# The last batch's contexts, output and writes stand behind the experts

## The chip, the cores and the metric

One core of a Trainium2 chip runs the whole program. The metric is device time in microseconds (us) of one execution; shown are the median of several executions and their range. One further execution was recorded by the hardware profiler, and every duration below comes from it. Engines: TensorE (PE) multiplies matrices, VectorE (DVE) and ScalarE (ACT) work on elements, GpSimd (POOL) here mostly issues indirect DMAs, SyncE (SP) issues the loads of weights. An indirect DMA takes or writes rows of a table in HBM by a list of row numbers; one form of it adds to the rows that are there.

## The reference

Four decoder layers on x of 8 batches with 100 tokens of 512 numbers, each layer an attention to a context of 361 tokens per batch and a feed-forward block. The change touches only the last layer, L3: a linear attention with 16 heads of 32, and 16 experts of inner size 352, four for each token. The expert numbers cover tokens 0 to 511 only, so the tokens from 512 on get nothing from the experts.

```python
q_prime = relu(einsum('bhnd,fd->bhnf', q, Wqf))
k_prime = relu(einsum('bhnd,fd->bhnf', k, Wkf)) * attention_mask[:, None, :, None]
kv  = einsum('bhnf,bhne->bhfe', k_prime, v)
qkv = einsum('bhmf,bhfe->bhme', q_prime, kv)
out = qkv / (einsum('bhmf,bhf->bhm', q_prime, sum(k_prime, axis=2))[..., None] + 1e-08)
x   = x + (out.transpose(0, 2, 1, 3).reshape(B, Sq, H) @ Wo.T + bo)
...
xs   = layernorm(x)[tok]                       # rows sorted by expert
down = (silu(xs @ gate[e].T) * (xs @ up[e].T)) @ down[e].T
x    = x + zeros.at[tok].add(down * w_sorted[:, None])
```

## The kernel before

x stays on the chip as seven tiles of 128 rows (800 tokens; the last tile has 32). Within a batch the rows are sorted by a key of the first layer, so `home` holds for each row the token it belongs to, and whatever leaves the chip by token is written by an indirect DMA, the helper `scatter` (line 2133). `home_far` holds the tokens of rows 600 to 639. Tokens 512 and up need no expert; as sorting stays within a batch, the first six batches (600 rows, `T3P`) hold all tokens that do. Row 600 lies in tile 4, whose first 88 rows (`NEAR`) belong to batch 5.

`linear_attention` runs a loop over the batches. In step b it makes keys and values of batch b (`kv_pieces`, 4 key and 3 value pieces), their features (`features`, VectorE operation kp, line 1858), and for batch b-1 `sums` (k'v and the sum of k'), `turned` (four transposes of it and a copy) and `attend`. `attend` is 64 small matmuls, then on VectorE an addition, a reciprocal and two products (lines 1919 to 1922), which overwrite qT with the contexts. After the contexts comes the product with the output weight `wo`, four products of 128 x 512 to a tile (the trace counts eight matmul records), and an addition to x (`out_to_x`, line 229). In step 7 the tiles of the first 512 rows get their output, then tile 4 for its first 88 rows only (`out_part(0)`; a column of ones and zeros decides which rows count, line 1942). `spread_normal` then normalises the five tiles into y and scatters y to the table `normal` in HBM, and x to the output. The buffers of y are two. A ninth step finishes batch 7 (turned, attend), the other 40 rows of tile 4 and tiles 5 and 6, and three scatters write them. All of the attention's TensorE work is held in the written order (`in_order`); other engines and DMAs are ordered by a planner, which puts what is ready first at the front of an engine's queue. Every queue then runs in order: an instruction that waits holds all behind it.

`routed_experts` goes over the 16 experts, `widen` of expert e+1 ahead of `narrow` of expert e. Each expert has 152 places in two halves of 76. `widen` loads the gate and up weights (704 KB each, line 90, four buffers `w`, shared with the attention's four weights), gathers the rows from `normal` by two indirect DMAs (xs, line 2163, three buffers), transposes them and makes 48 matmuls. `narrow` loads the down weight (768 KB, line 96, two buffers `v`), makes 48 matmuls, turns the result back, scales it (o, line 2213), and adds it to the output by two indirect DMAs with addition (line 2215). The two of one expert touch different rows; an expert's pair waits until the pair of the expert before has landed, since a token has several experts. A conditional block behind the experts handles more than 152 places of an expert.

Of the kernel before, what the change touches and what calls it, by code (L numbers as in the profile page):

```python
# [22 lines left out]
F32 = mybir.dt.float32  # L23
# [7 lines left out]
T = NB * LQ  # L31
# [28 lines left out]
def decoder_kernel(ctx: ExitStack, tc: tile.TileContext, a: dict, out: bass.AP):  # L60
# [50 lines left out]
    @contextmanager  # L111
    def in_order():
        pinned[0] = True
        yield
        pinned[0] = False
# [44 lines left out]
    NEAR = T3P - NT3 * 128  # L160
    assert T3P + 128 - NEAR <= T3P + LQ
    home_far = const.tile([128 - NEAR, 1], I32, name="home_far")

    def gather_x(src):
        for t, rows in TILES:
# [101 lines left out]
    def window_attention():  # L267
# [7 lines left out]
        with ExitStack() as st:  # L275
# [18 lines left out]
            with tc.tile_pool(name="l0s", bufs=1) as sp, tc.tile_pool(name="l0c", bufs=2) as cp, in_order():  # L294
# [141 lines left out]
                for t, rows in TILES:  # L436
# [5 lines left out]
                    p3[: 128 - NEAR, NTT : NTT + 1],  # L442
                    [(perm.rearrange("p b q -> p (b q)")[:, T3P : T3P + 128 - NEAR], iota_p[:LQ])],
                )
                ahead = sp.tile([128, NTT, NB - 1], F32, name="ahead")
                nc.gpsimd.iota(
                    ahead,
# [10 lines left out]
                nc.vector.tensor_tensor(home[:rows, t, :], batch[:rows, t : t + 1], p3[:rows, t : t + 1], ALU.add)  # L458
                nc.vector.tensor_scalar(
                    home_far, p3[: 128 - NEAR, NTT : NTT + 1], float(T3P), None, ALU.add  # L460
                )
                gather_x(a["x"])

# [1316 lines left out]

    def linear_attention(ctxT, first_done):

# [2 lines left out]
        F = 64  # L1789
        JP = KD // 2  # L1790
        halves = [slice(i * F, (i + 1) * F) for i in range(2)]
        with ExitStack() as st, in_order():
            res = st.enter_context(tc.tile_pool(name="a3", bufs=1))
            wq, wk, wv, wo = weights_of("a3_w")
            bqk = res.tile([128, 2, KD], F32, name="bqk")
# [3 lines left out]
            nc.sync.dma_start(out=feat, in_=a["a3_feat"])  # L1799
            mask = res.tile([128, NB, 3], F32, name="mask")  # L1800
            nc.sync.dma_start(out=mask, in_=a["mask_ff"])
            kvp = st.enter_context(tc.tile_pool(name="a3k", bufs=2))

            def of_head(m, g):

# [61 lines left out]
            def sums(b):  # L1867

                kp, va = kps.pop(b), kv.pop(b)[1]
                p = ps1()  # L1870
                n = KD * F
                for j in range(KD):
                    for c, (_, kn) in enumerate(KCH):
                        for g in range(4):
                            matmul(
                                p[four_heads(g), j * F : (j + 1) * F],
                                lhsT=va[:kn, c, j * 4 + g, :],
                                rhs=kp[:kn, c, g, j, :],
                                start=c == 0,
                                stop=c == 2,  # L1880
                            )
                for c, (_, kn) in enumerate(KCH):
                    for g in range(4):
                        matmul(
                            p[four_heads(g), n : 2 * n],
                            lhsT=ones[:kn, 0:HD],
                            rhs=kp[:kn, c, g, :, :].rearrange("p j f -> p (j f)"),
                            start=c == 0,
                            stop=c == 2,
                        )  # L1890
                sT = hp.tile([128, 4, 128], F32, name="sT")
                nc.scalar.copy(sT.rearrange("p i n -> p (i n)"), p)
                return sT

# [8 lines left out]
            def attend(b, z):  # L1903
                toks = slice(b * LQ, (b + 1) * LQ)
                p = ps2()
                for m in range(2):
                    for jp in range(JP):
                        for i, part in enumerate(halves):
                            for g in range(4):
                                c0 = (m * JP + jp) * LQ  # L1910
                                matmul(
                                    p[four_heads(g), i, c0 : c0 + LQ],
                                    lhsT=z[part, m, jp, four_heads(g)],
                                    rhs=qp[part, jp, g, toks],
                                    start=True,
                                    stop=True,
                                )
                rl = hp.tile([128, 2, JP * LQ], F32, name="rl")
                nc.vector.tensor_scalar(rl, p[:, :, JP * LQ : 2 * JP * LQ], 1e-8, None, ALU.add)
                nc.vector.reciprocal(rl, rl)  # L1920
                for i in range(2):
                    nc.vector.tensor_tensor(  # L1922
                        qT[:, i::2, toks],
                        p[:, i, : JP * LQ].rearrange("p (j q) -> p j q", j=JP),
                        rl[:, i, :].rearrange("p (j q) -> p j q", j=JP),
                        ALU.mult,
                    )
# [1 line left out]
            woks = [wo[:, k, :] for k in range(KD)]  # L1929


            counts = res.tile([128, 2], F32, name="counts")
            nc.gpsimd.iota(
                counts, pattern=[[0, 2]], base=-NEAR, channel_multiplier=1, allow_small_or_imprecise_dtypes=True
            )
            for i, op in enumerate((ALU.is_lt, ALU.is_ge)):
                nc.vector.tensor_scalar(counts[:, i : i + 1], counts[:, i : i + 1], 0.0, None, op)

            def out_part(i):
                p = ps1()  # L1940
                mm(p, [(qT[:, k, NT3 * 128 : NT3 * 128 + 128], w) for k, w in enumerate(woks)])
                nc.vector.scalar_tensor_tensor(
                    x[:, NT3, :], p, counts[:, i : i + 1], x[:, NT3, :], ALU.mult, ALU.add
                )

            for b in range(NB + 1):
                if 0 < b < NB:
                    kv[b] = kv_pieces(kvp, ctxT, b, wk, wv, bqk[:, 1, :], bv)
                keys, values = (kv[b][2][0::2], kv[b][2][1::2]) if b < NB else ([], [])
                if b == 0:  # L1950
                    keys = []
                    values[1:] = [lambda v=values[1:3]: (v[0](), due.pop()(), v[1]())]
# [3 lines left out]
                    sT = sums(b - 1)  # L1956
                if b == NB - 1:
                    out_to_x(qT, woks, TILES[:NT3])
                    out_part(0)
                    first_done()  # L1960
                if b == NB:
                    out_part(1)
                for part in keys[2:]:
                    part()
                if b:
                    z = turned(sT)
                for c in range(3):
                    if b < NB:
                        features(b, c)
                    for part in values[c : c + 1]:  # L1970
                        part()
                if b:
                    attend(b - 1, z)
            out_to_x(qT, woks, TILES[NT3 + 1 :])
            scatter(flat, home_far, x[NEAR:, NT3, :])
            for t, rows in TILES[NT3 + 1 :]:
                scatter(flat, home[:rows, t, :], x[:rows, t, :])

# [149 lines left out]
    def scatter(dst, at, src):  # L2130
# [5 lines left out]
        )  # L2136
        for other in writes[:-1]:
            tc.declare_no_dep(writes[-1].ins, other.ins, reason="each token has its own row")

    def spread_normal():  # L2140

        tiles = [(t, min(128, T3P - t * 128)) for t in range(NT3 + 1)]
        with tc.tile_pool(name="f3y", bufs=2) as yp:
            stats = norm_stats(x, NT3 + 1)
            for t, rows in tiles:
                y = yp.tile([128, D], F32, name="y")
                normed(y, x, stats, t)
                scatter(normal, home[:rows, t, :], y[:rows, :])
            for t, rows in tiles:
                scatter(flat, home[:rows, t, :], x[:rows, t, :])  # L2150

    def routed_experts():
        with ExitStack() as st:
            hp = st.enter_context(tc.tile_pool(name="f3h", bufs=2, reuse_waits="tile"))

            def widen(e):

                wg, wu = (
                    load_w(a["f3_gu"][e, i])[:, : KD * I3].rearrange("p (k n) -> p k n", k=KD) for i in range(2)
                )  # L2160
                xs = hp.tile([SH, 2, D], F32, name="xs", bufs=3)
                for h in range(2):
                    nc.gpsimd.indirect_dma_start(
                        out=xs[:, h, :],
                        out_offset=None,
                        in_=normal,
                        in_offset=bass.IndirectOffsetOnAxis(ap=r_tok[:, e, h : h + 1], axis=0),
                    )
                xT = hp.tile([128, KD, SLOTS], F32, name="xT")
                for h in range(2):  # L2170
                    p = ps1()
# [22 lines left out]
            def narrow(e, hT):  # L2194
# [11 lines left out]
                evac(oT.rearrange("p (i k) s -> p i (k s)", i=2), p[:, :, : 2 * SLOTS])  # L2206
                o = hp.tile([SH, 2, D], F32, name="o", bufs=4)
                adds = []
                for h in range(2):
                    p = ps1()  # L2210
                    for d in range(KD):
# [8 lines left out]
                            compute_op=ALU.add,  # L2220
                        )
                    )
                tc.declare_no_dep(adds[1].ins, adds[0].ins, reason="an expert's slots have different rows")

            skewed(range(E3), widen, narrow)


        with tc.If(nc.values_load(n_over, min_val=0, max_val=E3 * T3) > 0), ExitStack() as st:
            res = st.enter_context(tc.tile_pool(name="f3o", bufs=1))
            hp = st.enter_context(tc.tile_pool(name="f3p", bufs=2))  # L2230
# [43 lines left out]
            again()  # L2274

    window_attention()
    with ExitStack() as later:
        begun = []

        def follow(between):  # L2280
# [6 lines left out]
        ctxT = begun[0]  # L2287
        softmax_attention(ctxT)
        gated_ffn()
        linear_attention(ctxT, spread_normal)  # L2290
    routed_experts()

# [137 lines left out]
```

## Time and profile before

| what | us |
|---|---|
| median of 3 runs (range) | 2076.41 (2071.13 to 2076.53) |
| profiled execution, device time | 2075.22 |
| its span, first to last instruction | 2073.4 |
| TensorE busy in the span | 1903.3 (92%) |
| VectorE, ScalarE, GpSimd busy | 834.3, 523.5, 228.7 |
| last product of the attention ends (1846.41 + 8.80) | 1855.2 |
| first matmul of expert 0 | 1863.81 |
| last transposes of expert 15 begin | 2042.36 |
| indirect DMA with addition: from issue to landing, smallest, median, largest | 7.0, 7.9, 13.9 |
| gather of xs: from issue to landing, median | 6.8 |

Three views are used. The table by stage gives busy time of each engine in a stretch; it shows which engine is full and where none is. The timeline lists instructions with the idle time before them and what ended it. The chain of waits follows the last instruction back to what it waited for. A wait for several things is shown under the one that ended last.

### The profile page before, as it was taken

What the parts mean: (1) busy time and instruction counts of PE and PEld (TensorE: products, weight loads), DVE (VectorE), ACT (ScalarE), POOL (GpSimd) and SP (SyncE); (2) the same over time, 40 slices, a digit from 0 to 9 for tenths busy, and PEclk for the clock granted to TensorE, in tenths of its full rate; (3) what the DMA queues carried; (4) which work ended last, traced back from release to release, by engine and by line L of the source; (5) the groups of instructions that cost most, each with busy time, mean ns of one, the idle gap of its engine ahead of it and who ended that gap; (6) DMA issues with size and microseconds to landing.
All of it is one profiled execution on the core that took longest, in us unless ns stands there. A gap on an engine that the chain in (4) does not pass through costs nothing.

```text
span 2073.4 us, 28880 instructions
## 1 busy us (share of the span) xinstructions
PE 1903.3 (92%) x12202; PEld 1127.2 (54%) x12202; DVE 834.3 (40%) x1567; ACT 523.5 (25%) x1150; POOL 228.7 (11%) x197
## 2 busy tenths in 40 slices
PE   6999999889989999578999999999998999979993
PEld 4676665433345555234555554555444555539993
DVE  4354444543343364774455564111113333332221
ACT  1243323234214433262344441001001111001110
POOL 4100000123200000201000000000001000124452
PEclk8999999999989999799999999999998999989997
DMA  9600000468902221300000010111021000027883
GB/s 274 203 23 19 31 21 2 187 246 258 357 22 82 82 82 42 117 1 11 21 1 1 1 42 21 46 56 41 21 81 21 1 2 2 27 88 215 257 255 58
DMA packets 61565, 171.99 MB, mean 83 GB/s; under 512 B 18840, under 2 KB 27332, under 8 KB 54640
## 3 DMA queue, kind: packets, MB, share of 16 engines
q1 hardware_dynamic: 35122, 135.37, 18.8%
q0 software_dynamic: 21296, 25.42, 5.3%
q10 hardware_dynamic: 5006, 9.22, 1.3%
q8 instruction: 100, 1.64, 0.3%
q14 instruction: 41, 0.34, 0.1%
HBM read 146.10 MB, written 19.55 MB: 80 GB/s over the span
## 4 chain that ended last, share of the span: by engine, by line
PE 48%; issue 15%; DVE 8%; DMA 6%; ACT 3%; POOL 1%; POOLq 0%; DVEq 0%; ACTq 0%; SPq 0%
PE ps L102 45%; PE ps L107 3%; DMA out_x<-o,r_row 2%; ACT sc L1683 1%; DMA got<-back,where_i 1%; ACT pT L1425 1%; DMA read<-table 1%; DVE amax L1579 1%; DVE va L1299 1%; DMA ctxT<-in_ctxT 1%; DVE y L196 1%; DVE pT L1420 1%; DVE sc L1688 0%; POOL sent L1084 0%; DVE nmx L1680 0%
## 5 line engine op out<-in xcount | busy, mean ns | idle before, releaser
L102 PE MATMUL ps<-yT,w 128*128 128x400 f32 x768 | 267.1, 510 | 0.0
L102 PE MATMUL ps<-w,ctxT 128*128 128x512 f32 (+1 forms) x576 | 264.9, 603 | 0.0
L102 PE MATMUL ps<-ctxT,w 128*128 128x361 f32 x768 | 251.1, 475 | 0.0
L102 PEld LDWEIGHTS ps<-yT,w 128*128 128x128 f32 x768 | 148.5, 194 | 115.0 <-issue 8.6
L102 PEld LDWEIGHTS ps<-ctxT,w 128*128 128x128 f32 x768 | 142.3, 190 | 91.6 <-issue 17.5
L102 PEld LDWEIGHTS ps<-w,ctxT 128*128 128x128 f32 (+1 forms) x576 | 102.7, 184 | 118.6 <-issue 109.8
L1291 ACT ACTIVATE kT<-ps,bqk 128x361 f32<-128x361 f32 x96 | 53.6, 559 | 227.3 <-PE ps L102 226.1
L1299 DVE TENSOR_TENSOR va<-ps,r_a_bv 128x512 f32<-128x512 f32 (+1 forms) x72 | 49.7, 690 | 143.1 <-PE ps L102 143.1
L102 PE MATMUL ps<-xT,w 128*128 128x152 f32 (+1 forms) x768 | 104.4, 297 | 1.2 <-issue 0.6
L102 PEld LDWEIGHTS ps<-xT,w 128*128 128x128 f32 (+1 forms) x768 | 100.8, 183 | 2.6 <-issue 0.8
L229 DVE TENSOR_TENSOR x<-x,ps 128x512 f32<-128x512 f32 (+1 forms) x52 | 35.7, 686 | 138.9 <-PE ps L102 138.9
L102 PE MATMUL ps<-w_vo,oc 128*128 128x512 f32 (+1 forms) x224 | 90.5, 598 | 0.0
L917 DVE TENSOR_TENSOR hT<-sg,ps 128x400 f32<-128x400 f32 x36 | 20.6, 571 | 163.3 <-PE ps L102 161.1
L102 PE MATMUL ps<-w,qT 128*128 128x512 f32 (+1 forms) x176 | 79.0, 606 | 4.8 <-DVE qT L1922 4.8
L1683 ACT ACTIVATE sc<-ps,nmx 100x361 f32<-100x361 f32 x128 | 70.2, 561 | 50.2 <-DVE nmx L1680 50.2
L107 PEld LDWEIGHTS ps<-ident,sc 100*128 100x128 f32 (+1 forms) x512 | 54.5, 153 | 39.4 <-issue 25.1
L1425 ACT ACTIVATE pT<-pT,mbi,msc 128x800 f32<-128x800 f32 (+1 forms) x48 | 47.9, 1046 | 103.4 <-DVE pT L1420 103.4
L2215 POOL DMA_INDIRECT out_x<-o,r_row x32 | 59.0, 1844 | 100.2 <-DMA out_x<-o,r_row 58.0
L631 ACT ACTIVATE sc<-sc,nmx 100x128 f32<-100x128 f32 x128 | 49.8, 390 | 79.4 <-DVE nmx L628 78.4
L107 PE MATMUL ps<-ident,sc 100*128 100x100 f32 (+1 forms) x512 | 63.6, 261 | 5.3 <-DVE va L1299 3.9
L2119 POOL DMA_DIRECT2D read<-table x1 | 3.5, 3487 | 568.0 <-issue 568.0
L102 PE MATMUL ps<-v,hT 128*128 128x512 f32 (+1 forms) x140 | 61.8, 593 | 0.0
(377 smaller groups left out, 2763.9 us busy)
## 6 DMA issues: line engine op xcount, KB each, us to landing
w<-in_f_gu SPq DMA_DIRECT2D x32, 704.0 KB, 6.7
wd<-in_f_dn SPq DMA_DIRECT2D x32, 512.0 KB, 6.0
v<-in_f_w SPq DMA_DIRECT2D x16, 1024.0 KB, 6.0
w<-in_a_w SPq DMA_DIRECT2D x12, 1024.0 KB, 6.5
v<-in_f_dn SPq DMA_DIRECT2D x16, 768.0 KB, 8.7
w<-in_f_gu SPq DMA_DIRECT2D x9, 1024.0 KB, 4.8
gu<-in_f_gu SPq DMA_DIRECT2D x8, 1024.0 KB, 18.4
cx<-in_ctxT SPq DMA_DIRECT2D x8, 722.0 KB, 12.8
```

The costliest lines, as they stand in the source:

```text
L102: ins = nc.tensor.matmul(dst, **args)
L107: ins = nc.tensor.transpose(dst, src, unit)
L196: nc.vector.tensor_scalar(dst, src[:, t, :], mv[:, t, 0:1], rstd[:, t : t + 1], ALU.subtract, ALU.mult)
L229: nc.vector.tensor_tensor(x[:rows, t, :], x[:rows, t, :], p[:rows, :], ALU.add)
L631: nc.scalar.activation(sc[:, g, :], sc[:, g, :], AF.Exp, bias=nmx[:, g : g + 1], accum_out=l[:, g : g + 1])
L1291: ins = nc.scalar.activation(kT[:, m, :], p[:, :LK], AF.Identity, bias=bk[:, m : m + 1])
L1299: ins = nc.vector.tensor_tensor(va[:kn, c, :, 0:HD], p[:kn, :].rearrange("p (h d) -> p h d", d=HD), bv[:kn, :].rearrange("p (h d) -> p h d ...
L1420: nc.vector.tensor_scalar(dst, s[i][:kn, :, : KD * LQ], LIM * root, -LIM * root, ALU.min, ALU.max)
L1425: nc.scalar.activation(dst, dst, AF.Exp, bias=mbi[:kn, b, c : c + 1], scale=msc[:kn, b, c : c + 1])
L1579: nc.vector.tensor_reduce(amax, src, AX.X, ALU.max, apply_absolute_value=True)
L1683: nc.scalar.activation(sc[:, h, :], s[i][:LQ, g, :LK], AF.Exp, bias=nmx[:, g : g + 1], accum_out=l[:, h : h + 1])
L2215: nc.gpsimd.indirect_dma_start(out=flat, out_offset=bass.IndirectOffsetOnAxis(ap=r_row[:, e, h : h + 1], axis=0), in_=o[:, h, :], in_offse ...
```

## The change

1. The ninth step leaves the attention. A new function `rest` does batch 7's `turned` and `attend`, the rows of batch 7 in tile 5, tile 6, and their writes. It is called in `narrow` of expert 15, ahead of that expert's last transposes and adding writes. It loads `wo` a second time.
2. Tile 5 holds the end of batch 6 (rows up to 700, 60 rows of the tile: `HEAD`) and the beginning of batch 7. Its output product is now done twice, once for each part of the rows, as tile 4's already was, and it is written in two parts; `home_last` holds the tokens of the second part. One small matmul and one VectorE operation at the start make it; two more small columns choose the rows.
3. `sums` of batch 7, the second part of tile 4, the first part of tile 5 and their writes stay ahead of the experts.
4. The gathers of experts 0 and 1 are traced right after batch 6's contexts, ahead of these writes (`ask`). The gather of expert e+2 is traced in `widen` of expert e. xs has two buffers instead of three, in a pool opened before the attention.
5. y is written into the two buffers `v`, four tiles to a buffer, in place of two buffers of its own.
6. The pools move: the attention's tiles stay until the experts end; the pool of keys and values and the experts' pool lie on the other side of the memory, the latter where the context was. sT and rl have one buffer instead of two.
7. Dependencies: the moved writes and the adding writes are declared independent, as no expert's row is of the last batch; the last pair keeps its wait for the pair before it.

```diff
-            for b in range(NB + 1):
-                if 0 < b < NB:
+            for b in range(NB):
+                if b:
                     kv[b] = kv_pieces(kvp, ctxT, b, wk, wv, bqk[:, 1, :], bv)
...
-                    out_part(0)
+                    out_part(0, 0)
                     first_done()
-                if b == NB:
-                    out_part(1)
...
-            out_to_x(qT, woks, TILES[NT3 + 1 :])
+            ask()
+            sT = sums(NB - 1)
+            out_part(0, 1)
             scatter(flat, home_far, x[NEAR:, NT3, :])
-            for t, rows in TILES[NT3 + 1 :]:
-                scatter(flat, home[:rows, t, :], x[:rows, t, :])
+            out_part(1, 0)
+            scatter(flat, home[:HEAD, TL, :], x[:HEAD, TL, :])
+
+        def rest():
+            with in_order():
+                wo = load_w(a["a3_w"][3]).rearrange("p (k n) -> p k n", k=KD)
+                woks = [wo[:, k, :] for k in range(KD)]
+                attend(NB - 1, turned(sT))
+                out_part(1, 1, woks)
+                out_to_x(qT, woks, TILES[TL + 1 :])
+            done = [scatter(flat, home_last, x[HEAD:, TL, :])]
+            for t, rows in TILES[TL + 1 :]:
+                done.append(scatter(flat, home[:rows, t, :], x[:rows, t, :]))
+            return done
...
     def spread_normal():
-        with tc.tile_pool(name="f3y", bufs=2) as yp:
-            stats = norm_stats(x, NT3 + 1)
-            for t, rows in tiles:
-                y = yp.tile([128, D], F32, name="y")
+        stats = norm_stats(x, NT3 + 1)
+        two = [vpool.tile([128, 2048], F32, tag="v", name="v") for _ in range(2)]
+        for t, rows in tiles:
+            y = two[t // 4][:, t % 4 * D : (t % 4 + 1) * D]
...
-                xs = hp.tile([SH, 2, D], F32, name="xs", bufs=3)
-                for h in range(2):
-                    nc.gpsimd.indirect_dma_start(
...
+                xs = asked.pop(0)
+                if e + 2 < E3:
+                    asked.append(fetch(e + 2))
...
                 evac(oT.rearrange("p (i k) s -> p i (k s)", i=2), p[:, :, : 2 * SLOTS])
                 o = hp.tile([SH, 2, D], F32, name="o", bufs=4)
                 adds = []
+                others = rest() if e == E3 - 1 else []
...
+                    for other in others:
+                        tc.declare_no_dep(adds[h].ins, other.ins, reason="no expert's row is of the last batch")
+                        for before in all_adds[-2:]:
+                            tc.add_manual_dep(
+                                adds[h].ins,
+                                before.ins.name,
+                                mybir.DependencyInfo(mybir.DependencyClass.Sync, mybir.DependencyReason.DATA),
+                            )
...
-        linear_attention(ctxT, spread_normal)
-    routed_experts()
+        fetch = rows_of(last.enter_context(tc.tile_pool(name="f3x", bufs=2)))
+        asked = []
+        rest = linear_attention(ctxT, last, spread_normal, lambda: asked.extend(fetch(e) for e in range(2)))
+        later.close()
+        routed_experts(last, fetch, asked, rest)
```

`fetch(e)` allocates xs and issues the same two gathers as before.

## Prediction, made before the changed kernel was built

> **What bounds the kernel now.** I read the table by stage first, over the end of the last layer. Columns: stretch, its length, busy time of TensorE (PE) with count, weight loads, VectorE (DVE), ScalarE (ACT), GpSimd (POOL), granted TensorE clock, DMA share, GB/s.
>
> ```profile
> 1820.00:1840.00 20.00, 18.44 (x272) 9.82 (x273) 10.06 (x14) 0.58 (x1) 1.88 (x2) 0.91 0.18 60
> 1840.00:1860.00 20.00, 11.12 (x89) 4.37 (x87) 5.98 (x7) 0.61 (x2) 6.15 (x6) 0.91 0.21 64
> 1860.00:1880.00 20.00, 16.32 (x116) 16.03 (x117) 2.21 (x6) 3.29 (x7) 8.03 (x8) 0.83 0.51 154
> 1940.00:1960.00 20.00, 19.97 (x158) 19.59 (x158) 4.44 (x10) 2.47 (x7) 11.39 (x8) 1.00 0.87 240
> 2040.00:2060.00 20.00, 2.54 (x20) 2.05 (x18) 2.34 (x4) 0.00 (x0) 7.26 (x4) 0.69 0.24 33
> ```
>
> TensorE is full up to 1840, has a hole at the hand-over from attention to experts (1840 to 1864), is full again through the experts, and stands still from about 2043 while POOL goes on. So two places are open: the hole, and the tail. The timeline of the hole (start, duration, engine, line, operation, tiles, count, idle before and who ended it):
>
> ```profile
> 1815.30 0.55 DVE L196 TENSOR_SCALAR y<-x,mv,rstd 128x512 f32<-128x512 f32 x1 [2.72 <-DMA normal<-y,home]
> 1819.11 0.55 DVE L196 TENSOR_SCALAR y<-x,mv,rstd 128x512 f32<-128x512 f32 x1 [3.27 <-DMA normal<-y,home]
> 1820.37 0.44 PE L102 MATMUL ps<-feat,kT 32*128 32x64 f32 x4 [1.45 <-DVE kp L1858]
> ...
> 1836.68 3.70 PE L102 MATMUL ps<-w,qT 128*128 128x512 f32 x8 [0.97 <-DVE qT L1922]
> 1840.21 0.60 PE L107 MATMUL ps<-ident,sT 128*128 128x128 f32 x4
> 1846.41 8.80 PE L102 MATMUL ps<-w,qT 128*128 128x512 f32 x16 [3.85 <-DVE qT L1922]
> 1852.74 0.98 POOL L2133 DMA_INDIRECT out_x<-x,home  x1 [10.36 <-DVE x L229]
> 1854.02 1.16 POOL L2163 DMA_INDIRECT xs<-normal,r_tok  x1 [0.30 <-issue]
> 1862.45 0.74 PE L107 MATMUL ps<-ident,xs 76*128 76x76 f32 x4 [2.51 <-DMA xs<-normal,r_tok]
> ```
>
> The rows of the first expert are asked for only at 1854.02, behind a write that waited 10.36 us for x. Expert 0's first matmul follows at 1863.81. In the tail, POOL's timeline shows the pairs of adding writes (L2215), one pair per expert, and the chain of waits ends on them:
>
> ```profile
> 1909.19 1.86 POOL L2215 DMA_INDIRECT out_x<-o,r_row  x1 [6.29 <-DMA out_x<-o,r_row]
> 1923.88 1.86 POOL L2215 DMA_INDIRECT out_x<-o,r_row  x1 [7.78 <-DMA out_x<-o,r_row]
> 1939.36 1.87 POOL L2215 DMA_INDIRECT out_x<-o,r_row  x1 [8.58 <-DMA out_x<-o,r_row]
> 2051.44 1.82 POOL L2215 DMA_INDIRECT out_x<-o,r_row  x1 [6.33 <-DMA out_x<-o,r_row]
> 2062.22 1.84 POOL L2215 DMA_INDIRECT out_x<-o,r_row  x1 [6.84 <-DMA out_x<-o,r_row]
> ```
>
> Each expert's pair waits until the pair before has landed. The sixteen pairs start from 1884.81 to 2062.22: 15 periods in 177.4 us, mean 11.83. TensorE's period per expert is 11.0 (transposes of o at 1949.21, 1960.38, 1971.22). The periods after experts 1, 2 and 3 are 13.2, 14.7 and 15.5; from expert 4 on the mean is 11.2. So the pairs fall about 10 us behind o (o of expert 4 at 1927.81, its pair at 1939.36) and stay there. Call that lag D. At the end the adds alone last from 2043 to 2073.4. The end is therefore first pair + 15 periods + the last landing (2073.4 - 2062.2 = 11.2).
>
> **The change, part by part.**
>
> *The normalised rows.* y now has room for all five tiles, so the 2.72 and 3.27 us for which VectorE waited on a landed write go. Behind them in VectorE's queue stood kp, and for kp TensorE stood 1.45 + 0.22 us (1820.37, 1821.03). Gain 0 to 1.7; I take 1.5, as the row names the cause. The price: y borrows the two buffers in which the down weights of experts 0 and 1 were loaded long before. Both loads (768 KB each) now wait for the writes of normal, about 1822, land 9 to 11 us later, and are needed at 1879.06 - 20. The attention's last 20 us and expert 0 cover them: nothing. Without this cover one load, some 10 us, would show once.
>
> *The hole.* Four gathers (1.45 us apart on POOL) now stand behind the writes of normal (last issued 1821.74, landed some 3.2 us later), so about 1825 to 1831. A gather lands in 4.8 us on a quiet DMA and at worst 12.1 in this trace: 1843 at the latest. POOL's writes of x behind them wait for VectorE until 1841 anyway. TensorE keeps its work up to the half product ending at 1840.3, adds the half of the tile in which batch 7 begins (8 matmuls, 3.70) up to 1844.0, and transposes the rows at once; from the second transposes to the first matmul it was 1.36 (1862.45 to 1863.81). First matmul of expert 0: 1845.4 instead of 1863.81, **18.4 earlier**. If the gathers stood behind the write waiting for 1841.47, they would land near 1849 and 5 of it were lost. The second weight of expert 1 waits for the buffer of the output weight, issued at 1855.24; its buffer now comes free at 1844, 11 earlier, and lands 6.7 later, before expert 1 at about 1853. Expert 0's matmuls took 7.84 at clock 0.83, later ones 6.44: with a shorter hole 0 to 1.4 come back; I take 0.6. So the first pair of adds moves by 18.4 + 1.5 + 0.6 = **20.5**; bounds 13 and 21.5.
>
> *Two buffers of rows instead of three.* The gather for expert e+2 now needs the buffer of expert e, free after its transposes. On POOL it stands behind the pair of e-2, as the gather for e+3 does now (1896 pair 1, 1900.30 gather for 6 by the three buffers). What is queued behind the waiting pair is thus the gather for four experts later, and TensorE waits for it. Its second half starts 4.3 + 1.45 us after the pair begins and lands after L. The rows are wanted two periods and 0.35 after o: slack = 22.65 - 1.05 - D - 5.75 - L = 15.8 - D - L. L has medians of 5.6 to 10 in windows over the experts. With D = 10 and L = 7 the slack is -1.2: TensorE will stall a little at most experts from about the eighth on. That alone costs nothing, since the pairs, not o, set the end; it lowers D. But D fixes where a pair falls against the burst of weight loads: pairs starting 2.9 to 4.2 us after a burst (bursts at 1935.13, 1946.35, 1968.37) had periods of 10.3 to 11.9, those near its start (1923.88 against 1924.28) 15.5. Cost: from nothing to 12 periods at 13 (+22); I take +0.4 for eight periods, **+3**, being nearest to the rows at 2.9.
>
> *The work behind the experts.* Transposes, contexts and two output tiles lasted 1840.21 to 1856.0, 15.8 us, most of it waiting (reciprocal 2.65, clock 0.82 in the 8.80). It is the same work plus, on POOL, one more write than before (0.95 + 0.3): tile 5 is written in two parts, and two writes stand ahead of the last pair. It begins after expert 15's last product, 2041.4 on the old clock, and its writes are issued by 2041.4 + 15.8 + 2 = 2059.2. The last pair waits for its forerunner until 2062.2. So 3 us of cover are left, and TensorE's stalls come off it: 0 to 5; I take 0.5. The second load of the output weight (1 MB, 6.5 us) takes the buffer that comes free at 2024: 10 us early, nothing. Without the lag D, these 15.8 us would all stand on the path.
>
> *At the start* one more matmul and one VectorE operation, and a few on small tiles: 0 to 0.4 us, I take 0.2.
>
> **A rule against it.** For a SWDGE transfer (issued by GpSimd) the Trainium skill, "DMA: Bandwidth & Descriptors", section "Anatomy of one DMA — SWDGE (gpsimd) path", gives 2.0 us plus bytes over 436 GB/s. For 76 rows of 2 KB that is an estimate of 2.4 us. The pairs here land in 7.0 to 13.9 us, median 7.9. By the rule pairs would never lag, the cover in the tail would not exist, and the end would be o of expert 15 plus the 15.8 us: the moved work would come back in full, and of the gain 20.5 - 15.8 - 2 = 2.7 us would be left. The measurement decides here.
>
> **The sum.** Span 2073.4 - 20.5 + 3 + 0.5 + 0.2 = 2056.6. The profiled execution took 2075.22, so 1.8 lie around the span, and the median of the runs is 2076.41, 1.2 above it: **2060**. Own range 2052 to 2068.
>
> **The rivals.**
> - *The pairs stop lagging.* In an undisturbed order the periods equal TensorE's 11.0 from the start, and the tail is TensorE's: 2041.4 - 20.5 + 15.8 + 2 + 11.2 = 2049.9, with 3.0 around it 2053. For it: expert 4's pair and later have 11.2. Against: three of the first four periods are long. Chance 0.12.
> - *The gathers come late at the start, and the moved work shows in the tail.* 13 instead of 20.5 gained, 5 exposed: 2073.4 - 13 + 3 + 5 + 3 = 2071; it does only half of what it says. For it: POOL's queue is in order, and here a write waiting for x held the gathers. Against: nothing they need is later than 1825. Chance 0.12; half of it lies within the noise.
> - *Slower: the two buffers tie TensorE to the adds.* Each gather sits behind a pair that waits for a landing; if stalls pull D down to 6, pairs meet the weight bursts and the period stays at the 13.2 to 15.5 of experts 1 to 3. At a mean of 14.2 the 15 periods take 213 instead of 177.4: 2073.4 - 20.5 + 35.6 + 3 = 2091.5. It decides from a mean period of (177.4 + 20.5 + 6.2)/15 = 13.6. Against: a longer period leaves the DMA more time between bursts, and shortens L. Chance 0.11.
>
> **How the numbers follow.** Forecast 0.65, the others 0.12, 0.12, 0.11. A measurement tells about 0.3% (6 us) from no change. Faster: 0.65 + 0.12 + 0.06, less 0.03 for the forecast's own longest stalls, 0.80; within 0.3% 0.09; slower 0.11. The range runs from 2051 to 2076: below it lies part of the first rival, above it the slower one and the worst of the second.
>
> **What would show it.** Right: the first gather issued before 1835 and the first expert's matmul at 1842 to 1847; no VectorE wait on the writes of normal; TensorE waiting 0.5 to 3 us for xs at several later experts; pairs with a mean period of 11.5 to 12.2; the contexts, output and three writes done before the last pair. Wrong: gathers behind the write to out_x at 1841; mean periods above 13; the last pair waiting for VectorE or for the moved writes instead of for its forerunner. What would break the forecast is the phase of adds against weight loads, which I only read from single periods.

## The result, and the profile after

The changed kernel is faster by 0.7%: median 2056.66 us (2052.87 to 2068.04, 10 runs) against 2076.1 (2064.31 to 2077.41, 10 runs) of the kernel before. The ratio is 0.9934, with a 95% interval of 0.9912 to 0.9956. The profiled execution has a span of 2051.1 (before 2073.4), 22.3 less.

The table by stage of the changed kernel (columns as before):

```profile
1820.00:1840.00 20.00, 18.75 (x254) 9.80 (x253) 8.91 (x12) 1.37 (x3) 5.77 (x6) 1.00 0.52 154
1840.00:1860.00 20.00, 19.15 (x154) 18.85 (x155) 3.10 (x8) 3.39 (x8) 5.31 (x6) 1.00 0.69 227
1860.00:1880.00 20.00, 20.00 (x159) 19.66 (x157) 4.54 (x10) 2.40 (x7) 11.87 (x8) 1.00 0.71 191
2020.00:2040.00 20.00, 11.16 (x24) 4.10 (x24) 6.52 (x8) 0.00 (x0) 7.50 (x5) 0.82 0.26 42
```

The hole at 1840 to 1864 is gone: TensorE is busy 19.15 of 20 us there, at clock 1.00 instead of 0.91 and 0.83. The work that stood in it now shows in 2020 to 2040. The timeline of the hand-over:

```profile
1810.53 2.53 DVE L199 TENSOR_SCALAR v<-x,mv,rstd 128x512 f32<-128x512 f32 x5
1820.96 1.17 POOL L2186 DMA_INDIRECT xs<-normal,r_tok  x1 [3.25 <-issue]
1826.99 1.02 PE L102 MATMUL ps<-qp,z 64*32 64x100 f32 x64
1831.76 7.13 PE L102 MATMUL ps<-w,qT 128*128 128x512 f32 x16 [0.60 <-DVE qT L1933]
1836.57 0.95 POOL L2160 DMA_INDIRECT out_x<-x,home_far  x1 [10.14 <-DVE x L1955]
1838.73 0.69 PE L107 MATMUL ps<-ident,xs 76*128 76x76 f32 x8
1840.24 6.44 PE L102 MATMUL ps<-xT,w 128*128 128x152 f32 x48 [0.81 <-ACT xT L85]
```

The five normalisations run in one go, the gathers go out at 1820.96 (before 1854.02), ahead of the write that waits 10.14 us for x, and expert 0 starts at 1840.24 (before 1863.81). The tail:

```profile
2018.85 1.02 PE L102 MATMUL ps<-qp,z 64*32 64x100 f32 x64 [0.68 <-ACT z L1911]
2023.63 10.16 PE L102 MATMUL ps<-w,qT 128*128 128x512 f32 x16 [3.76 <-DVE qT L1933]
2027.04 1.81 POOL L2256 DMA_INDIRECT out_x<-o,r_row  x1 [7.41 <-DMA out_x<-o,r_row]
2031.33 1.10 POOL L2160 DMA_INDIRECT out_x<-x,home_last  x1 [0.36 <-DVE x L1955]
2034.50 1.39 DVE L2254 TENSOR_SCALAR o<-ps,r_wgt 76x512 f32<-76x512 f32 x2
2034.85 0.89 POOL L2160 DMA_INDIRECT out_x<-x,home  x1 [2.43 <-DVE x L232]
2038.07 1.88 POOL L2256 DMA_INDIRECT out_x<-o,r_row  x1 [2.32 <-DMA out_x<-o,r_row]
```

The moved work lies between the pairs of experts 14 (2027.04) and 15 (2038.07). o of expert 15 is delayed to 2034.50, yet its pair still waits 2.32 us for a landing: that of the pair before it.

What lies ahead of the change varies from profile to profile: the first write of x to the output falls at 1794.0 to 1808.4 in the fourteen profiles. So below, times marked "counted" are counted from that write; before it nothing in these kernels differs but a few small instructions. "Lag" below is the time from the beginning of an expert's o to its pair, less the 1.0 to 1.1 us that a pair takes that waits for nothing else (seen at most experts of after_plain).

| kernel | median us | ratio to before (95%) | first pair, counted | 15 periods | end, counted |
|---|---|---|---|---|---|
| before | 2076.1 | | 88.5 | 177.4 | 277.1 |
| changed | 2056.66 | 0.9934 (0.9912 to 0.9956) | 64.6 | 178.2 | 255.9 |
| rest_ahead | 2071.92 | 0.9996 (0.9968 to 1.0023) | 80.1 | 176.4 | 269.7 |
| gathers_behind | 2066.55 | 0.9963 (0.9937 to 0.9989) | 74.9 | 180.4 | 268.3 |
| rows_three | 2052.8 | 0.9899 (0.9854 to 0.9945) | 64.8 | 176.3 | 254.1 |
| y_two | 2058.31 | 0.9933 (0.9903 to 0.9962) | 68.3 | 181.6 | 262.9 |
| rest_left_out | 2058.42 | 0.9936 (0.9907 to 0.9966) | 64.8 | 178.3 | 256.1 |
| before_plain | 2056.5 | 0.9929 (0.9899 to 0.9959) | 90.5 | 160.9 | 259.4 |
| after_plain | 2043.72 | 0.9868 (0.9821 to 0.9914) | 64.8 | 173.5 | 245.7 |
| rest_last | 2053.85 | 0.9922 (0.9884 to 0.9961) | 64.7 | 177.9 | 255.0 |
| no_weight_loads | 2049.95 | 0.9881 (0.9832 to 0.9929) | 64.8 | 174.4 | 251.9 |
| no_gathers | 2052.25 | 0.9887 (0.9838 to 0.9936) | 64.8 | 176.0 | 254.1 |
| three_and_last | 2061.3 | 0.9947 (0.9919 to 0.9974) | 72.6 | 176.0 | 261.1 |
| three_later_last | 2053.8 | 0.9904 (0.9886 to 0.9923) | 65.5 | 175.2 | 253.2 |

The kernel before stands in each comparison on the same chip; its medians there are 2073.2 to 2076.1, its single runs 2058 to 2086. The medians of different comparisons can differ by some us for that reason alone.

### The profile page after: what moved, and what is told of

Read it like the earlier page. It is cut to its first block, busy times and chain, and to the rows that moved or that the text cites. A ratio compares the mean times of both kernels' runs of the same rounds, so it can differ in the third digit from the quotient of the medians.

```text
span 2051.1 us, 28912 instructions
## 1 busy us (share of the span) xinstructions
PE 1902.6 (93%) x12212; PEld 1125.5 (55%) x12212; DVE 834.2 (41%) x1571; ACT 523.3 (26%) x1150; POOL 232.0 (11%) x199
## 3 DMA queue, kind: packets, MB, share of 16 engines
q1 hardware_dynamic: 35266, 136.42, 19.4%
## 4 chain that ended last, share of the span: by engine, by line
PE 60%; DVE 8%; DMA 7%; ACT 3%; issue 2%; POOL 1%; POOLq 0%; DVEq 0%; ACTq 0%; SPq 0%
PE ps L102 56%; PE ps L107 3%; DMA v<-in_f_dn 2%; DMA out_x<-o,r_row 2%; ACT sc L1693 1%; ACT pT L1435 1%; DVE amax L1589 1%; DVE va L1309 1%; DMA read<-table 1%; DVE y L199 1%; DVE pT L1430 1%; DMA got<-back,where_i 0%; DMA ctxT<-in_ctxT 0%; DVE sc L1698 0%; DVE nmx L1690 0%
## 5 line engine op out<-in xcount | busy, mean ns | idle before, releaser
L102 PE MATMUL ps<-w_vo,oc 128*128 128x512 f32 (+1 forms) x224 | 90.5, 598 | 0.0
L102 PE MATMUL ps<-w,qT 128*128 128x512 f32 (+1 forms) x184 | 83.8, 613 | 4.4 <-DVE qT L1933 4.4
L927 DVE TENSOR_TENSOR hT<-sg,ps 128x400 f32<-128x400 f32 x36 | 20.5, 571 | 163.3 <-PE ps L102 158.4
L1869 DVE TENSOR_SCALAR kp<-ps,mask 128x512 f32<-128x512 f32 (+1 forms) x48 | 33.9, 746 | 73.7 <-PE ps L102 70.5
```

What stands on the lines that cost most here:

```text
L102: ins = nc.tensor.matmul(dst, **args)
L1869: nc.vector.tensor_scalar(kps[b][:kn, c, 2 * i : 2 * i + 2, :, :].rearrange("p g j f -> p g (j f)"), s[i][:kn, :, : KD * F], 0.0, mask[:kn ...
```

## The experiments: where the gain comes from

**rest_ahead.** The last batch ahead of the experts again.

```diff
+        rest()
         later.close()
         routed_experts(last, fetch, asked, rest)
...
-                others = rest() if e == E3 - 1 else []
+                others = []
```

(`rest` here uses the output weight that is already loaded.)

> The changed kernel, but the last batch's transposes, contexts, output and writes stand ahead of the experts again, with the output weight that is already there; the early gathers, y in the weight buffers and the two buffers of rows stay. Theory (the moved work is hidden behind the lagging pairs of adding writes): expert 0's first matmul comes 13 to 15 us later than the 1840.24 of the changed kernel, the tail is set by the pairs as before, so the span is 13 to 15 us longer than 2051.1, about 2065. Rival (the moved work is paid in the tail): no longer than the changed kernel, within 4 us.

```profile
1844.98 9.50 PE L102 MATMUL ps<-w,qT 128*128 128x512 f32 x16 [3.85 <-DVE qT L1933]
1855.77 6.44 PE L102 MATMUL ps<-xT,w 128*128 128x152 f32 x48 [0.61 <-ACT xT L85]
```

The moved products stand ahead of expert 0 again, which starts at 1855.77 instead of 1840.24. The first pair comes 15.5 us later than the changed kernel's (80.1 against 64.6), the end 13.8 later; the medians differ by 15.3. The theory holds: the moved work costs about its whole length at the hand-over and little in the tail. Against the kernel before, the profile's end is 7.4 earlier counted, while the timed ratio is 0.9996, between a gain of 0.3% and a loss of 0.2%. So what is left without the move (early gathers, y in one go) is 0 to 7 us; the runs don't settle it closer.

**gathers_behind.** The first four gathers held behind the two writes of x.

```diff
-            ask()
             sT = sums(NB - 1)
...
             scatter(flat, home[:HEAD, TL, :], x[:HEAD, TL, :])
+            ask()
```

(Each of these gathers also keeps the written order on GpSimd.)

> The changed kernel, but the gathers for experts 0 and 1 are held behind the two writes of x that precede the experts. Theory (the place of the gathers in GpSimd's queue is worth what they come later): the write of tile 5's first rows goes out at about 1840, the second half of expert 0's rows lands at about 1847.5, its first matmul at about 1849, 8 to 9 us later than in the changed kernel, and the span grows by the same 8 to 9. Rival (the first expert waits for something else anyway, a weight for instance): under 3 us.

Timeline of this kernel (its first write is at 1799.06, 3.8 later than in the changed kernel):

```profile
1843.87 0.91 POOL L2160 DMA_INDIRECT out_x<-x,home  x1 [2.59 <-DVE x L1955]
1845.08 1.17 POOL L2186 DMA_INDIRECT xs<-normal,r_tok  x1 [0.30 <-issue]
1850.32 0.74 PE L107 MATMUL ps<-ident,xs 76*128 76x76 f32 x4 [7.60 <-DMA xs<-normal,r_tok]
```

TensorE stands 7.60 us for the rows, and its granted clock falls: expert 0's 48 matmuls take 7.82 us at 0.82 where the changed kernel's take 6.44 at 1.00. The first pair is 10.3 later counted; the medians differ by 9.9. The place in the queue is worth 8.9 us at the first matmul (counted 53.9 against 45.0), as expected, and 1.4 more through the clock. The losses of rest_ahead and gathers_behind can't be added up: together they exceed the 19.4 us by which the medians of the two kernels differ, since each run takes away a part on which the gain of the other rests.

**y_two.** y with two buffers of one tile each.

```diff
-        two = [vpool.tile([128, 2048], F32, tag="v", name="v") for _ in range(2)]
         for t, rows in tiles:
-            y = two[t // 4][:, t % 4 * D : (t % 4 + 1) * D]
+            y = vpool.tile([128, 2048], F32, tag="v", name="v")[:, :D]
```

> The changed kernel, but y has only two buffers again (one tile of it in each of the two weight buffers), so that the normalisation waits for landed writes. Theory (VectorE's queue held kp, kp held TensorE, and the pauses also lowered the clock): the stretch from the half output to batch 6's contexts grows by 3 to 4 us, and the span by as much. Rival (the prediction's step): 1.5 us. Second rival: nothing, the waits are hidden.

```profile
1825.86 0.55 DVE L199 TENSOR_SCALAR v<-x,mv,rstd 128x512 f32<-128x512 f32 x1 [3.10 <-DMA normal<-v,home]
1826.32 1.40 DVE L1869 TENSOR_SCALAR kp<-ps,mask 128x512 f32<-128x512 f32 x2
1827.12 0.44 PE L102 MATMUL ps<-feat,kT 32*128 32x64 f32 x4 [1.29 <-DVE kp L1869]
1828.82 5.40 PE L102 MATMUL ps<-w,ctxT 128*128 128x512 f32 x8
```

The old pattern is back: a wait for a landed write, kp behind it, TensorE behind kp, and then eight matmuls in 5.40 us at a granted clock of 0.68 that take 3.70 at 1.00 in the changed kernel. Counted, batch 6's contexts start at 35.5 instead of 31.8, and the first pair at 68.3 instead of 64.6: 3.7 us. The timed ratios are the same to 0.0001, with intervals of 0.2 and 0.3% (5 and 6 us) to each side: the times neither show the 3.7 us nor exclude them, and only the profile shows them at their place.

**rows_three.** Three buffers of rows in the loop, five experts' rows asked for at the start. The buffers from expert 2 on lie with the experts' other tiles.

```diff
-                if e + 2 < E3:
-                    asked.append(fetch(e + 2))
+                for n in ((2, 3) if e == 0 else (e + 3,)):
+                    if n < E3:
+                        asked.append(fetch(n, hp, bufs=3))
```

> The changed kernel, but with five buffers' worth of rows at the start and three in the loop (the gather for expert e+3 instead of e+2). Theory after the profile of the changed kernel, in which TensorE never waits for xs: within 2 us of the changed kernel. Rival (the prediction's step): the two buffers cost 3 us or more, so this is 3 us or more faster.

No wait of TensorE for xs, and the end counted is 1.8 earlier, within the theory's 2; the ratio of 0.9899 leans further, but the intervals overlap. In other kernels with two buffers TensorE does wait now and then: 1.67 us once in gathers_behind, 3.54 once in y_two, 1.01 and 1.15 in rest_left_out. So two buffers cost 0 to 4 us; closer the runs don't say.

## The experiments: why the tail hides the moved work

**rest_left_out.** The moved contexts and products are left out; batch 7's rows are written without their attention.

```diff
-            with in_order():
-                wo = load_w(a["a3_w"][3]).rearrange("p (k n) -> p k n", k=KD)
...
-                attend(NB - 1, turned(sT))
-                out_part(1, 1, woks)
-                out_to_x(qT, woks, TILES[TL + 1 :])
```

(The second load of the output weight goes with them.)

> The changed kernel without the last batch's transposes, contexts and output product behind the experts (the rows of batch 7 leave without their attention; the writes stay). Theory (hidden behind the lagging pairs): o of expert 15 comes 16 us earlier, but its pair still waits for the pair before it; counted from the first write of x, the end comes 0 to 3 us earlier than the changed kernel's 255.9 where the pairs lag by about 10 us. Rival (the moved work is on the path): 10 us earlier or more.

```profile
2018.87 1.40 DVE L2248 TENSOR_SCALAR o<-ps,r_wgt 76x512 f32<-76x512 f32 x2 [0.73 <-PE ps L107]
2026.16 1.82 POOL L2250 DMA_INDIRECT out_x<-o,r_row  x1 [8.23 <-DMA out_x<-o,r_row]
2037.06 1.84 POOL L2250 DMA_INDIRECT out_x<-o,r_row  x1 [6.96 <-DMA out_x<-o,r_row]
```

o of expert 15 comes at 2018.87, and its pair still goes out only at 2037.06, a lag of 17.1 us, as its forerunner lands. The end counted is 256.1, against 255.9 with the work. The work is free where it stands.

**before_plain and after_plain.** In both kernels the experts' results are written plainly instead of added, so a row holds one expert's result.

```diff
                             in_=o[:, h, :],
                             in_offset=None,
-                            compute_op=ALU.add,
```

> The kernel before, with the experts' results written plainly instead of added (so rows hold one expert's result alone). Theory (the lag comes from the landing of the adding writes): pairs land in some 3 us, as the plain writes of x do, no pair lags, and the end is o of expert 15 plus about 9 us: some 20 us shorter than before. Rival (the lag comes from GpSimd's issue or from the waits themselves): within 5 us of before.

> The changed kernel with the same plain writes. Theory: without the lag the moved work stands on the path, o of expert 15 at about 239 us from the first write of x and the end at about 248; against the kernel before with plain writes only some 8 us are gained instead of 21. Rival (the moved work is hidden by something other than the lagging pairs): 18 us or more are gained over the plain kernel before.

The tails of the two, POOL's timeline, first before_plain, then after_plain:

```profile
2040.96 1.13 POOL L2215 DMA_INDIRECT out_x<-o,r_row  x1 [8.28 <-DVE o L2213]
2042.40 1.14 POOL L2215 DMA_INDIRECT out_x<-o,r_row  x1 [0.30 <-issue]
2047.66 1.13 POOL L2215 DMA_INDIRECT out_x<-o,r_row  x1 [4.12 <-DMA out_x<-o,r_row]
```

```profile
2013.63 1.12 POOL L2256 DMA_INDIRECT out_x<-o,r_row  x1 [8.30 <-DVE o L2254]
2028.22 1.10 POOL L2160 DMA_INDIRECT out_x<-x,home_last  x1 [12.04 <-DVE x L1955]
2032.91 1.12 POOL L2256 DMA_INDIRECT out_x<-o,r_row  x1 [0.30 <-DVE o L2254]
```

With plain writes the lag is at most 0.7 us up to expert 14: it takes adding writes to make it. Without it the kernel before is 17.7 shorter counted. Then the moved work shows: expert 15's pair follows expert 14's by 19.3 us instead of 6.7, and the pair waits for o, not for a landing. The end counted gains 259.4 - 245.7 = 13.7 instead of 21.2. It is more than the 8 expected, since the first pair moves by 25.7 here and 12.6 come back. A plain pair lands in some 5 us (2042.40 to 2047.66), not in 3.

**no_weight_loads and no_gathers.** These ask what makes the adding writes late: all experts use the weights, or the rows, of experts 0 and 1 in turn.

```diff
+                if e < 2:
+                    held[e] = [
+                        load_w(a["f3_gu"][e, i])[:, : KD * I3].rearrange("p (k n) -> p k n", k=KD) for i in range(2)
+                    ]
+                wg, wu = held[e % 2]
...
-                xs = asked.pop(0)
-                if e + 2 < E3:
-                    asked.append(fetch(e + 2))
+                xs = asked[e % 2]
```

(the first block, and the same for the down weights, in no_weight_loads; the second in no_gathers)

> The changed kernel, with the weights of experts 0 and 1 used for all experts in turn, so that no expert's weights are loaded after the second. Theory (the weight loads stretch the landings of the adding writes, and so make the periods of 14 to 16 us and the lag): every pair lands in about 7 us as in the quiet tail, no period is over 12.5, the lag stays under 2 us up to expert 14, and the last pair is late only by the moved work. Rival (the gathers that follow each pair on the same queue stretch them): a lag of 6 us or more builds up in the first ten experts as before.

> The changed kernel, with the rows of experts 0 and 1 used for all experts in turn, so that no gather runs beside the pairs. Theory (the weight loads do it): two periods of 13 us or more and a lag of 8 to 11 us remain. Rival (the gathers do it): no period over 12.5 and a lag under 2 us.

Without gathers the lag is there as before: periods of 14.4 and 14.3, then 8.5 to 10.5 us of lag up to expert 14. Without weight loads the lag stays at 1.2 us or less up to expert 11; against the expectation one period of 14.2 comes near the end, and the lag is 5.4 us at experts 13 and 14. The timeline of no_weight_loads shows what lies there:

```profile
1995.24 1.86 POOL L2260 DMA_INDIRECT out_x<-o,r_row  x1 [5.31 <-DMA out_x<-o,r_row]
1997.41 1.83 POOL L2260 DMA_INDIRECT out_x<-o,r_row  x1 [0.30 <-issue]
1999.05 0.33 SPq L90 DMA_DIRECT2D w<-in_a_w  x1
2009.41 1.82 POOL L2260 DMA_INDIRECT out_x<-o,r_row  x1 [10.18 <-DMA out_x<-o,r_row]
```

It is the only weight load left in that stretch, the second load of the output weight, 1.6 us behind the pair's second issue. The pair's period is 14.2 where its neighbours have 12.2 and 10.9. So a single weight load can make a long period. It matters when it starts. In the twelve profiles with adding writes, 22 of the 180 periods have an expert's first load of gate and up weights, or this one, starting 0.2 to 4.9 us behind the pair's first issue: they last 12.6 to 16.8 us, median 14.7. Of the others, save the last period of no_weight_loads, which waits for the moved work, all but five last 10.3 to 12.8, median 11.3, also where the load starts 5.1 us behind the issue or later, with the pair still in flight. The five last 13.0 to 13.9; one of them is the period after expert 1 in the kernel before, so this is not the whole cause. In the changed kernel the lag begins at experts 8 and 9:

```profile
1951.01 1.86 POOL L2256 DMA_INDIRECT out_x<-o,r_row  x1 [5.29 <-DVE xT L83]
1966.67 1.87 POOL L2256 DMA_INDIRECT out_x<-o,r_row  x1 [8.77 <-DMA out_x<-o,r_row]
1981.11 1.87 POOL L2256 DMA_INDIRECT out_x<-o,r_row  x1 [7.55 <-DMA out_x<-o,r_row]
```

with loads starting at 1955.56 and 1966.98, 4.5 and 0.3 us behind the pairs at 1951.01 and 1966.67. What is lost there is not won back: a lag of 8.5 to 11 us stays from expert 10 to 14. It began at experts 1 to 3 in the kernel before, 8 and 9 here, 2 in rows_three: where it starts differs, but it came in every profile with adding writes and weight loads.

## The experiments: what is left

**rest_last.** The moved work behind the last pair.

```diff
-                others = rest() if e == E3 - 1 else []
...
                 all_adds.extend(adds)
+                for other in rest() if e == E3 - 1 else []:
+                    for add in all_adds:
+                        tc.declare_no_dep(other.ins, add.ins, reason="no expert's row is of the last batch")
```

> The changed kernel, but the moved work stands behind expert 15's last transposes and its pair of adding writes instead of ahead of them. Theory (the last pair has a cover of only 1 to 4 us behind the moved work): the pair's o comes 16 us earlier, the pair itself only as its forerunner lands, the two writes go out while it lands: 1 to 3 us faster than the changed kernel, more in executions in which the pairs lag little. Rival (the writes behind the last pair now end last): slower by 2 us or more.

The last pair has a lag of 17.7 us, the writes go out at 2044.01 and 2045.42 behind the pair's second issue at 2041.89 and add nothing. The end counted is 0.9 earlier; the ratio, 0.9922, has an interval that holds the changed kernel's ratio. It is not slower; by the medians it is 2.8 us faster, which the spread doesn't confirm.

**three_and_last.** rows_three and rest_last together.

> The changed kernel with three buffers of rows and with the moved work behind the last pair. Theory (each takes away what is left of its wait: short stalls of TensorE on late rows, 1 to 3 us, and the last pair's thin cover): 2 to 5 us faster than the changed kernel, ratio to the kernel before 0.988 to 0.992. Rival (both are hidden behind the pairs): within 1.5 us of the changed kernel.

A miss on both sides: median 2061.3. The loss is at the hand-over, in TensorE's timeline:

```profile
1828.96 1.31 PE L102 MATMUL ps<-qp,z 64*32 64x100 f32 x48
1830.61 0.38 PE L102 MATMUL ps<-qp,z 64*32 64x100 f32 x5 [0.34 <-issue]
1831.37 0.40 PE L102 MATMUL ps<-qp,z 64*32 64x100 f32 x5 [0.38 <-issue]
1833.62 0.45 PE L102 MATMUL ps<-kp,va 128*32 128x64 f32 x5 [0.43 <-issue]
```

For 8 us small matmuls come in groups of about five with pauses in which TensorE waits for nothing that the profile shows; expert 0 starts at 53.0 counted instead of 45.2. rows_three has the same ten early gathers and no such pauses.

**three_later_last.** The same with the gathers of experts 2 to 4 held behind the writes of x.

> The kernel with three buffers of rows and the moved work behind the last pair, but with the gathers for experts 2 to 4 held behind the two writes of x, so that only four gathers run beside the end of the attention, as in the changed kernel. Theory (the ten early gathers go together with the 8 us of short pauses in TensorE's stream that the kernel without this hold showed): attend of batch 6 and sums run without pauses, expert 0's first matmul is back at about 45 us from the first write of x, and the median is 2 to 5 us below the changed kernel's, ratio 0.988 to 0.992. Rival (the pauses come from where the code lies, whatever the gathers do): the pauses stay, first matmul at 50 us or later, ratio 0.993 or more.

The pauses are gone, the first matmul is at 45.1, the end counted at 253.2, the earliest of the kernels that compute the whole, and the median is 2053.8, ratio 0.9904 (0.9886 to 0.9923). That is 2.7 us ahead of the changed kernel counted and 2.9 in the medians; the intervals of the ratios overlap, so it beats the kernel before for certain and the changed kernel probably. The hold removed the pauses here, but rows_three didn't need it: what they are stays open.

## Why the prediction was right

2060 was forecast and 2056.66 measured, for the reasons given: the hole closes, and the moved work hides behind the lagging pairs. The closeness of the number is partly luck. The profiled span is 2051.1 where the sum gave 2056.6; but that execution was the fastest of the ten, 3.8 us below the median, where the sum put the median 1.2 above it. Nor does the time alone tell the forecast from the first rival's 2053; the last pair's wait for its forerunner does. Counted from the first write of x:

- *The normalised rows*: 1.5 taken, bounds 0 to 1.7; 3.7 measured (y_two). The term was too small: I took TensorE's two waits from the rows and not the eight matmuls behind them, which took 5.40 at a clock of 0.69 instead of 3.70.
- *The hole*: 18.4; measured 67.5 - 45.0 = 22.5 to expert 0's first matmul, of which 3.8 came with batch 6's contexts, so 18.7. TensorE did not wait for the gathers. gathers_behind shows the loss if they had not: 8.9 at the first matmul, where 5 was named.
- *Expert 0's clock*: 0.6; 1.4 measured, the upper bound (21.0 to 19.6 from first matmul to first pair). The first pair moved by 23.9 instead of 20.5, outside the bounds of 13 to 21.5.
- *Two buffers of rows*: 3 taken; the fifteen periods are 0.8 longer and TensorE never waited for xs in that profile, nor did the lag stand at 10 us from expert 4 on: it came at expert 8. The stalls foreseen do occur, in three other profiles, at 1.0 to 3.5 us. The term is right in kind, and 3 was too much for this execution. The phase of pairs against weight loads, which the prediction had from single periods, is borne out: over all profiles most long periods go with loads starting 0.2 to 4.9 us behind the pair.
- *The work behind the experts*: 15.8 us with 3 us of cover, 0.5 taken. The work took 17.0 (2017.58 to the end of the last addition to x, 2034.57), and rest_left_out shows it hidden: 0.2 us of difference at the end. The last pair had a lag of 2.5 us left. The chain was that of the prediction.
- *Not foreseen*: the stretch from the last pair to the end took 13.0 instead of 11.2. It is 13.1 in rest_ahead and 13.0 in rest_left_out too, so it is not the moved work. In the traces the packets of the last pair take 8.2 to 8.3 us from first to last in these three and 6.5 in the kernel before, which is the difference; why they do stays open.
- *The sum*: 23.9 - 0.8 - 1.8 = 21.3, which is 277.1 - 255.9 = 21.2 within rounding; another 1.05 of the span's 22.3 lies ahead of the first write.

The first rival (pairs that do not lag) was right on TensorE's part for eight experts, then the lag came. The second fell with the first gather at 1820.96. The slower one never came near: its mean period of 13.6 compares with at most 12.1 in any run (181.6/15, y_two). The rule that was weighed against the change does not hold for these transfers: its estimate of 2.4 us stands against 7.0 to 13.9 for the adding writes and some 5 for plain ones. Its consequence is right where pairs don't lag: with plain writes the moved work does come back, 12.6 us of it.

## What to carry to other kernels

Where a chain of dependent transfers sets the end, the engine that feeds it has free time at the very end, and independent work put there is hidden up to the chain's lag; ahead of the chain the same work costs its whole length. Measure that lag (each transfer's start against its input) before relying on it, and check that the transfers stay slow: the cover here took adding writes and weight loads together, and with one of the two taken away (after_plain, no_weight_loads) the last pair waited for the moved work. An early request counts only if nothing that waits stands before it in its queue (8.9 us in gathers_behind); and behind a pause add what the engine's clock loses after it (1.4 us there).

## What the runs showed that was not expected

- A single 1 MB load, started 3.8 us behind a pair's first issue, went with a period of adding writes of 14.2 us instead of about 11 (no_weight_loads), and the lag so made does not shrink. Where an expert's loads start 5.1 to 6.3 us behind it, the period is 10.3 to 12.2 in 51 of 52 cases.
- Plain indirect writes of 76 rows by the same instructions leave a lag of at most 0.7 us up to expert 14; the kernel before is 17.7 us shorter counted with them.
- TensorE's pauses of 0.3 to 0.4 us every five or so small matmuls, over a stretch of 8 us, in one kernel (three_and_last) and not in two near relatives.
- The stretch ahead of the change ends between 1794.0 and 1808.4 us in the profiles, in kernels that hardly differ there. Differences of 2 to 4 us are seen in a profile counted from a common instruction, and not in the timed runs.
